# A routed convolution's first two images: sums by identity products, a residual by accumulating transfers, and another order on VectorE

## The chip, the cores and the metric

The kernel runs on one core of a Trainium2 chip. The metric is the device time of one execution in microseconds (us). A core has TensorE (PE, matrix products into PSUM, with PEld for its weight loads), VectorE (DVE), ScalarE (ACT), GpSimd (POOL) and SyncE (SP, here only an issuer of transfers). Each takes its instructions in the order of the program and waits for others on semaphores. Transfers are done by 16 DMA engines that all queues share.

## The reference

Eight images of 128 channels and 64 by 64 pixels go through two layers with residuals. Layer 0 is a modulated deformable 3x3 convolution, batch normalisation and a rectifier. Layer 1, which the change is about, is this:

```python
# --- layer 0 (conv_preact) ---
x = x + _L0_conv_ref(_gn(x), ...)          # ends in relu(yn * gamma + beta)
# --- layer 1 (conv_preact) ---
x = x + _L1_conv_ref(_gn(x), ...)

def _L1_conv_ref(x, ...):
    pooled = jnp.mean(x, axis=(2, 3))
    scores = jax.nn.sigmoid(pooled @ gate_w.T + gate_b)
    ...                                     # top 2 of 4 experts, weights to sum 1
    out = jnp.einsum('ebchw,be->bchw', ye, w_dense)   # ye: a 3x3 convolution by each expert
    return out + _conv2d(x, shared_w) + shared_b[None, :, None, None]
```

The group normalisation `_gn` has 32 groups of 4 channels. As the experts are linear, the kernel mixes their weights per image instead of their outputs, and runs one 3x3 convolution.

## The kernel before

Channels lie on the 128 partitions. `dense()` computes layer 0 band by band and stores its raw output y in DRAM. `layer1()` then goes over the images. Both fix the order of the instructions by hand (`manual_schedule`): what is written first comes first on its engine. SP's and POOL's instructions at the seam of the two layers are also in that order, with loads of layer 1 placed among the last stores of layer 0.

For image b, `load(b)` fetches y and the input x in four quarters each, into one of two pairs of buffers (x1 and xt; for even b the padded images of layer 0 serve). `prepare(b)` is a generator that makes all that the products of image b need, in this order:

- For eight chunks of 512 pixels: the batch normalisation's affine and rectifier on ACT (line 1101), the addition of xt (line 1103; on POOL, and for image 0 the odd chunks on DVE), and the chunk's statistics on DVE (`bn_stats`, line 1105).
- The statistics together (`mv`, line 1110), the group sums as two small products on PE (`pm` line 1113, `pv` line 1123), the scale by a power on POOL, and the gate: a small product `pg` (line 1145) and some fifteen small operations on DVE that end in the experts' weights `wd` (line 1176) and the mixed bias `bmix` (lines 1178 to 1181). Meanwhile ACT writes the normalised chunks into the padded image pad2 (line 1136).
- The mixed weights `wmix` on DVE (line 1212), and u1 and u2 from them (lines 1223 to 1225). The convolution is cut along rows by a transform that computes two output rows from four products (j = 0 to 3): products 0 and 3 use wmix itself, products 1 and 2 use u1 and u2.
- The transformed input v for four groups of 16 rows: transform 1 (line 1191), transform 2 (line 1193), each 528 elements a partition, and transform 0 (line 1195), 1056 elements. Image 0 does its first group's transforms 1 and 2 on POOL.

The main loop runs four products of three matrix products each per group (line 1275, each 128x512 in fp32, two records in the profile), and `collect` takes each result from PSUM: product 1 on ACT, the others on DVE, and a store of 512 KB per group on SP. The 48 matrix products of an image are PE's work of about 42 us. Between the products, `next(ahead_of)` advances `prepare(b + 1)` by one of its turns, nine turns a group. Image 0 is prepared in full before its first product is written down. So DVE does all transforms of image 0, then the statistics of image 1, and the small product pm of image 1 stands on PE's queue behind six products of group 1. For image 0 the first twelve matrix products go column by column of the kernel (kx), each after the weights of its column.

Of the kernel before, what the change touches and what calls it, by code (L numbers as in the profile page):

```python
# [8 lines left out]
F32 = mybir.dt.float32  # L9
I32 = mybir.dt.int32  # L10
AF = mybir.ActivationFunctionType
# [5 lines left out]
P = 128  # L17
# [40 lines left out]
def deform_moe_conv(  # L58
# [104 lines left out]
    most = const.tile([P, B], F32, name="most")  # L163

# [3 lines left out]
    def dense():  # L168

        with ExitStack() as st:  # L170
# [24 lines left out]
            ident = a1.tile([P, P], F32, name="ident")  # L195
# [615 lines left out]
    def general():  # L811

        with ExitStack() as st:
# [12 lines left out]
            ident = a1.tile([P, P], F32, name="ident")  # L826
            make_identity(nc, ident)
# [199 lines left out]
    def layer1():  # L1027
# [6 lines left out]
        with ExitStack() as st:  # L1034
# [8 lines left out]
            ident = b1.tile([P, P], F32, name="ident")  # L1043
            nc.gpsimd.memset(ident, 1.0)
            nc.gpsimd.affine_select(
                out=ident, in_=ident, compare_op=ALU.is_equal, fill=0.0, base=0,
                pattern=[[-1, P]], channel_multiplier=1,
            )
# [13 lines left out]
            def load(b):  # L1062
                if b >= B:
                    return
                x1, xt = x1s[b % 2], xts[b % 2]
                for q in range(4):
                    part = slice(q * HW // 4, (q + 1) * HW // 4)
                    nc.sync.dma_start(out=x1[:, part], in_=ydram[b][:, part])
                    nc.sync.dma_start(out=xt[:, part], in_=x[b, :, part])
                loaded[b] = x1, xt  # L1070
# [22 lines left out]
            def prepare(b, made):  # L1093
# [4 lines left out]
                for c in range(NCH + 2):  # L1098
                    if c < NCH:
                        y = x1[:, c * CH : (c + 1) * CH]  # L1100
                        nc.scalar.activation(y, y, AF.Relu, bias=yshift, scale=yscale)  # L1101
                        adder = nc.gpsimd if b or c % 2 == 0 else nc.vector
                        adder.tensor_tensor(y, y, xt[:, c * CH : (c + 1) * CH], ALU.add)  # L1103
                    if c > 1:
                        nc.vector.bn_stats(  # L1105
                            stats[:, c - 2, :], x1[:, (c - 2) * CH : (c - 1) * CH]
                        )
                    yield
                mv = small.tile([P, 2], F32, name="mv")
# [25 lines left out]
                def normalise(c):  # L1135
                    nc.scalar.activation(
                        pad2[:, 1 + 8 * c : 9 + 8 * c, 1 : W + 1],
                        x1[:, c * CH : (c + 1) * CH].rearrange("p (h w) -> p h w", w=W),
                        AF.Identity, bias=shift, scale=scale,
                    )  # L1140
# [36 lines left out]
                mb = small.tile([P, NE], F32, name="mb")  # L1177
                nc.vector.tensor_tensor(mb, eb_sb, wd, ALU.mult)
                bmix = small.tile([P, 1], F32, name="bmix")
                nc.vector.tensor_reduce(bmix, mb, AX.X, ALU.add)  # L1180
                nc.vector.scalar_tensor_tensor(bmix, bmix, sb_sb, gm, ALU.add, ALU.add)
# [21 lines left out]
                if b == 0:  # L1203
                    for c in range(4, NCH):
                        normalise(c)
                    transform(0, 1, nc.gpsimd)
                    transform(0, 2, nc.gpsimd)

                for kx in range(3) if b == 0 else (slice(0, 3),):
# [16 lines left out]
                    if kx == 0:  # L1226
                        transform(0, 0, nc.vector)
                    yield
                for g in range(NG):
                    if b or g:  # L1230
                        transform(g, 1, nc.vector)
                        transform(g, 2, nc.vector)
                        yield
                        transform(g, 0, nc.vector)
                        yield
                made[b] = vs, (wmix[:, 0], u1, u2, wmix[:, 2]), bmix

            made, todo = {}, []
            for _ in prepare(0, made):
                pass  # L1240
            for b in range(B):
                load(b + 2)
                ahead_of = prepare(b + 1, made) if b + 1 < B else iter(())
                vs, us, bmix = made.pop(b)
                for g in range(NG):
                    yo = b2.tile([P, TR, 2, W], F32, name="yo")
                    part = {}

                    def collect(j, pc, g=g, b=b, yo=yo, part=part, bmix=bmix):
# [10 lines left out]
                        elif j == 0:  # L1260
                            nc.vector.tensor_tensor(yo[:, :, 0], pc, part["s"], ALU.add)
                        else:
                            nc.vector.tensor_tensor(yo[:, :, 1], part["d"], pc, ALU.subtract)  # L1263
                            n = 2 * TR * W
                            nc.sync.dma_start(
                                out=out[b, :, g * n : (g + 1) * n],
                                in_=yo.rearrange("p t i w -> p (t i w)"),
                            )
# [13 lines left out]
                    if b == g == 0:  # L1282

                        pcs = {j: ps_m.tile([P, TR, W], F32, name="pc") for j in order}
                        for kx in range(3):
                            for j in order:
                                product(j, kx, pcs[j])
# [73 lines left out]
```

## Time and profile before

| | us |
|---|---|
| Median of three runs (1677.96 to 1679.51) | 1678.17 |
| The profiled execution | 1679.23 |
| Its span, first to last instruction | 1677.5 |
| TensorE busy in it | 1575.5 (94%) |
| End of layer 0's last product | 1293.25 |
| First product of layer 1 | 1320.22 |
| End of the last product | 1670.57 |

A row of a timeline reads: start, duration, engine, line of the code, operation, output and inputs by the program's names, shapes, count, and in brackets how long the engine was idle before it and what ended that. In a name such as `pad` or `x` the buffers of image 0 and image 1 can be told: image 0 lies in layer 0's `pad`, image 1 in `x` and `xt`. A table of waits gives total, times and the longest. A row of the windows gives the stretch, its length, busy time of PE, PEld, DVE, ACT and POOL, the granted TensorE clock as a share of full speed, the DMA engines' busy share and GB/s.

### The profile page before, as it was taken

Reading aid. Unit: us, or ns where it says so; the run is one execution under the profiler, and the core shown is the slowest. Engines: PE = TensorE matmul, PEld = TensorE weight load, DVE = VectorE, ACT = ScalarE, POOL = GpSimd, SP = SyncE. Lnnn points to the kernel's source line nnn. Section 1 sums busy time; section 2 is a strip of 40 time slices with the busy share of each in tenths; the row PEclk is TensorE's granted clock in tenths of the full one; section 3 lists DMA queues with packets and bytes.
Section 4 is the critical chain, followed back from the end, with each engine's and each line's share of the span. In section 5 each row is a group of like instructions: output and inputs, shape, how many; then the busy total and the mean of one; then the engine's idle time right before and its main releaser. Section 6 shows DMA issues by size and latency. Waiting matters only on the chain. (4 is left out here: it accounts for less than half of the span.)

```text
span 1677.5 us, 20746 instructions
## 1 busy us (share of the span) xinstructions
PE 1575.5 (94%) x6106; PEld 922.9 (55%) x6106; DVE 1089.8 (65%) x2150; ACT 903.9 (54%) x2096; POOL 956.1 (57%) x1519
## 2 busy tenths in 40 slices
PE   3399999999999999999999999999998489999998
PEld 1265665666566566656665665666665234444443
DVE  5565675666565656756665657565443988888882
ACT  2565764766575557647655755576564333333320
POOL 3475685678577666856775776677771412222210
PEclk9599999999999999999999999999999689999999
DMA  4654863785487468637854874666661634433111
GB/s 135 141 128 104 191 160 97 158 195 135 102 182 173 108 133 202 143 94 157 195 133 103 172 184 116 135 162 152 163 146 48 268 121 150 152 152 145 71 62 53
DMA packets 195668, 235.81 MB, mean 141 GB/s; under 512 B 131765, under 2 KB 146097, under 8 KB 195549
## 3 DMA queue, kind: packets, MB, share of 16 engines
q0 software_dynamic: 94768, 124.63, 33.1%
q1 hardware_dynamic: 100047, 109.38, 21.9%
q8 instruction: 53, 0.87, 0.2%
q14 instruction: 66, 0.54, 0.1%
q10 hardware_dynamic: 734, 0.39, 0.1%
HBM read 183.00 MB, written 50.82 MB: 139 GB/s over the span
## 5 line engine op out<-in xcount | busy, mean ns | idle before, releaser
L663 PE MATMUL pq<-s,xt 100*128 100x324 f32 (+2 forms) x1936 | 677.1, 431 | 18.6 <-DVE s L642 17.7
L678 ACT COPY samples<-pq 128x324 f32<-128x324 f32 (+5 forms) x1144 | 430.6, 400 | 453.8 <-PE pq L663 446.0
L642 DVE TENSOR_TENSOR s<-xwts,ywts 100x324 f32<-100x324 f32 x968 | 452.4, 491 | 318.7 <-PE pq L663 281.7
L689 PE MATMUL py<-samples,dw_sb 128*128 128x384 f32 (+1 forms) x1584 | 629.0, 479 | 6.1 <-ACT y L700 6.0
L588 POOL DMA_DIRECT2D xwts<-tabx x862 | 540.6, 636 | 94.9 <-DMA ywts<-taby 33.6
L572 POOL DMA_DIRECT2D ywts<-taby x526 | 302.3, 587 | 280.3 <-DVE s L642 235.7
L663 PEld LDWEIGHTS pq<-s,xt 100*128 100x128 f32 x1936 | 325.5, 191 | 181.9 <-issue 42.4
L689 PEld LDWEIGHTS py<-samples,dw_sb 128*128 128x128 f32 x1584 | 299.8, 190 | 130.3 <-ACT y L700 13.9
L625 PE MATMUL pt<-ident,picked 128*100 128x128 f32 x968 | 193.2, 275 | 19.7 <-ACT picked L612 19.7
L625 PEld LDWEIGHTS pt<-ident,picked 128*100 128x100 f32 x968 | 124.3, 129 | 146.2 <-issue 67.4
L1275 PE MATMUL pc<-v,u 128*128 128x512 f32 x384 | 172.8, 599 | 9.3 <-DVE u L1224 9.3
L1275 PE MATMUL pc<-v,wmix 128*128 128x512 f32 x384 | 176.6, 606 | 0.0
L632 ACT COPY xt<-pt 100x512 f32<-100x512 f32 (+1 forms) x264 | 147.5, 559 | 1.5 <-PE pt L625 1.4
L703 DVE BATCH_NORM_STATS2 ystats<-y 128x6 f32<-128x384 f32 (+1 forms) x88 | 48.2, 548 | 136.6 <-ACT y L700 136.6
L1275 PEld LDWEIGHTS pc<-v,u 128*128 128x128 f32 x384 | 72.7, 191 | 98.1 <-issue 85.4
L1275 PEld LDWEIGHTS pc<-v,wmix 128*128 128x128 f32 x384 | 72.7, 192 | 88.9 <-issue 85.3
L1253 ACT ACTIVATE t<-pc,bmix 128x512 f32<-128x512 f32 x32 | 22.0, 687 | 183.3 <-PE pc L1275 101.3
L1103 POOL TENSOR_TENSOR x<-x,xt 128x512 f32<-128x512 f32 x32 | 46.5, 1482 | 86.0 <-ACT x L1101 86.0
L604 ACT COPY picked<-pad 128x900 f32<-128x900 f32 x88 | 91.3, 1037 | 4.0 <-DMA xwts<-tabx 4.0
L322 DVE TENSOR_TENSOR combo<-pad 128x1024 f32<-128x1024 f32 x64 | 77.0, 1219 | 17.2 <-PE pc L339 9.7
L1103 POOL TENSOR_TENSOR pad<-pad,pad 128x512 f32<-128x512 f32 x28 | 39.5, 1437 | 71.7 <-ACT pad L1101 71.5
L779 DVE COPY samples<-samples 128x1188 f32<-128x1188 f32 x80 | 61.3, 767 | 0.0
(151 smaller groups left out, 1034.5 us busy)
## 6 DMA issues: line engine op xcount, KB each, us to landing
ywts<-taby POOLq DMA_DIRECT2D x526, 116.0 KB, 4.1
pad<-in_x_dram SPq DMA_DIRECT2D x48, 512.0 KB
xwts<-tabx POOLq DMA_DIRECT2D x172, 116.0 KB, 3.8
out_dram<-yo SPq DMA_DIRECT2D x32, 512.0 KB
xwts<-tabx POOLq DMA_DIRECT2D x173, 92.8 KB, 3.8
yd<-y SPq DMA_DIRECT2D x80, 192.0 KB
xwts<-tabx POOLq DMA_DIRECT2D x172, 69.6 KB, 3.7
pad<-yd SPq DMA_DIRECT2D x16, 512.0 KB
```

Source lines behind the costliest of these rows:

```text
L322: nc.vector.tensor_tensor(combo_of[j][:, half * n : half * n + n], *rows, op)
L572: engine.dma_start(out=y_wts[g % 2][r * Q : (r + NR) * Q, r].rearrange("p a b c -> p (a b c)"), in_=bass.AP(tensor=y_table[b].tensor, offs ...
L588: engine.dma_start(out=x_wts[g % 3][q:QQ:Q, :, lo:hi].rearrange("p t a b c -> p t (a b c)"), in_=bass.AP(tensor=x_table[b].tensor, offset= ...
L604: nc.scalar.copy(picked[g % 2][:, 1 : NT1 - 1], bass.AP(tensor=one.tensor, offset=one.offset, ap=[list(one.ap[0]), [T, NT1 - 2], [W, Q], [ ...
L625: nc.tensor.transpose(pt[0:QQ, c], picked[g % 2][:, c0 + c].rearrange("p y x -> p (y x)"), ident,)
L632: nc.scalar.copy(xts[g][0:QQ, c0 : c0 + n], pt[0:QQ, 0:n])
L642: nc.vector.tensor_tensor(s[0:QQ], x_wts[g % 3][0:QQ, c].rearrange("p a r (y x) -> p (r y) a x", x=3), y_wts[g % 2].rearrange("p r y a x - ...
L663: nc.tensor.matmul(pq[asked], lhsT=xts[g][0:QQ, c], rhs=ss.pop(n)[0:QQ].rearrange("p m a x -> p m (a x)")[asked], start=True, stop=True,)
L678: nc.scalar.copy(rows[:, 6 + m0 : 6 + m1, x, T * c + lo : T * c + hi], by_columns[:, m0:m1, x, lo:hi],)
L689: nc.tensor.matmul(py[:, first:], lhsT=dw_sb[:, 3 * ky + kx], rhs=samples[g % 2][:, first + ky : T + ky, 2 - ky, 2 - kx, kx : kx + W], sta ...
L1103: adder.tensor_tensor(y, y, xt[:, c * CH : (c + 1) * CH], ALU.add)
L1275: nc.tensor.matmul(pc, lhsT=us[j][:, kx], rhs=vs[g][:, rows, kx : kx + W], start=(kx == 0), stop=(kx == 2),)
```

## The change

- Layer 1 uses layer 0's identity matrix (now in the constants) and builds none of its own.
- Image 0: chunks 2, 4, 6 and 7 are summed on PE, as a product of the identity with xt and one with the rectified chunk, in PSUM; the statistics and the normalisation read them there. Chunks 0, 1, 3 and 5 are added on DVE. POOL adds none.
- Image 1: x is not loaded into xt; after each pair of rectified chunks POOL issues a transfer that adds x to them in place. All eight statistics come in one place, before group 2's transforms of image 0.
- Image 0's first group: transform 0 on POOL, 1 and 2 on DVE; the first twelve products go in the order 0, 3, 1, 2.
- bmix is computed after the weights.
- Image 0's `prepare` is not run to its end: the transforms of groups 2 and 3 are dealt out between image 1's turns (`merged`).
- The loads of image b + 2 are issued in group 1, not ahead of group 0.
- The very last store is split in two halves, the second issued from ACT.

```diff
+    ident = const.tile([P, P], F32, name="ident")
...
                     nc.sync.dma_start(out=x1[:, part], in_=ydram[b][:, part])
-                    nc.sync.dma_start(out=xt[:, part], in_=x[b, :, part])
+                    if b != 1:
+                        nc.sync.dma_start(out=xt[:, part], in_=x[b, :, part])
...
-                for c in range(NCH + 2):
-                    if c < NCH:
-                        y = x1[:, c * CH : (c + 1) * CH]
-                        nc.scalar.activation(y, y, AF.Relu, bias=yshift, scale=yscale)
-                        adder = nc.gpsimd if b or c % 2 == 0 else nc.vector
-                        adder.tensor_tensor(y, y, xt[:, c * CH : (c + 1) * CH], ALU.add)
-                    if c > 1:
-                        nc.vector.bn_stats(
-                            stats[:, c - 2, :], x1[:, (c - 2) * CH : (c - 1) * CH]
+                if b == 0:
+                    relus = list(chunks)
+                    summed = (2, 4, 6, 7)
+                    for c in summed:
+                        pc = ps_m.tile([P, TR, W], F32, name="pc")
+                        chunks[c] = pc.rearrange("p h w -> p (h w)")
+                        nc.tensor.matmul(
+                            chunks[c], lhsT=ident, rhs=xt[:, c * CH : (c + 1) * CH],
+                            start=True, stop=False,
                         )
+                    for c in range(NCH):
+                        nc.scalar.activation(
+                            relus[c], relus[c], AF.Relu, bias=yshift, scale=yscale
+                        )
+                        if c in summed:
+                            nc.tensor.matmul(
+                                chunks[c], lhsT=ident, rhs=relus[c], start=False, stop=True
+                            )
+                    for c in (0, 1, 3, 5):
+                        add(c, nc.vector)
+                        for done in {1: (0, 1), 3: (2, 3), 5: (4, 5, 6, 7)}.get(c, ()):
+                            count(done)
+                elif b == 1:
+                    for c in range(NCH):
+                        relu(c)
+                        if c % 2:
+                            part = slice((c - 1) * CH, (c + 1) * CH)
+                            nc.gpsimd.dma_start(
+                                out=x1[:, part], in_=x[b, :, part], accum_op=ALU.add
+                            )
                     yield
+                    for c in range(NCH):
+                        count(c)
+                        if c % 2:
+                            yield
...
-                    transform(0, 1, nc.gpsimd)
-                    transform(0, 2, nc.gpsimd)
+                    transform(0, 0, nc.gpsimd)
...
                     if kx == 0:
-                        transform(0, 0, nc.vector)
+                        transform(0, 1, nc.vector)
+                        transform(0, 2, nc.vector)
                     yield
+                mb = small.tile([P, NE], F32, name="mb")
...
+                made[b] = vs, (wmix[:, 0], u1, u2, wmix[:, 2]), bmix
                 for g in range(NG):
...
+            def merged(first, then):
+                wait = None,
+                turns = 2 * wait + (then,) + wait + 2 * (first,) + 5 * wait + 2 * (then,)
+                for turn in turns + 2 * wait + (then,) + 2 * (first,):
+                    if turn:
+                        next(turn)
+                    yield
+                yield from then
...
-            for _ in prepare(0, made):
-                pass
+            first = prepare(0, made)
+            while 0 not in made:
+                next(first)
+            next(first)
             for b in range(B):
-                load(b + 2)
                 ahead_of = prepare(b + 1, made) if b + 1 < B else iter(())
+                if b == 0:
+                    for _ in range(5):
+                        next(ahead_of)
+                    ahead_of = merged(first, ahead_of)
...
+                    if g == 1:
+                        load(b + 2)
...
+                            halves = 2 if b == B - 1 and g == NG - 1 else 1
+                            m = TR // halves
...
-                            for j in order:
+                            for j in (0, 3, 1, 2):
                                 product(j, kx, pcs[j])
```

## The prediction

> **What bounds the kernel now.** I read the page's head first, then the waits of TensorE from 1290 us on, then the timelines of the engines between the two layers, then windows for clock and transfers.
>
> ```profile
> span 1677.5 us, 20746 instructions
> PE 1575.5 (94%) x6106; PEld 922.9 (55%) x6106; DVE 1089.8 (65%) x2150; ACT 903.9 (54%) x2096; POOL 956.1 (57%) x1519
> ```
>
> TensorE (PE) is the bound almost everywhere; what can be won is its idle time. The order of instructions of layer 0 is the same in both kernels, so only the time after 1293 us counts. Who PE waits for there (total, times, longest):
>
> ```profile
> PE pm L1113 <- DVE mv L1110: 23.6, 2, 14.2
> PE pc L1275 <- DVE u L1224: 9.3, 1, 9.3
> ```
>
> The 23.6 us are two waits for statistics: image 0's (14.2) and image 1's. PE's timeline:
>
> ```profile
> 1307.41 0.58 PE L1113 MATMUL pm<-mv,gsel 128*128 128x1 f32 x2 [14.16 <-DVE mv L1110]
> 1320.22 3.75 PE L1275 MATMUL pc<-v,u 128*128 128x512 f32 x4 [9.29 <-DVE u L1224]
> 1326.25 1.88 PE L1275 MATMUL pc<-v,u 128*128 128x512 f32 x4
> 1333.14 5.31 PE L1275 MATMUL pc<-v,u 128*128 128x512 f32 x12
> 1347.90 0.59 PE L1113 MATMUL pm<-mv,gsel 128*128 128x1 f32 x2 [9.44 <-DVE mv L1110]
> 1392.32 0.28 PE L1113 MATMUL pm<-mv,gsel 128*128 128x1 f32 x2
> ```
>
> Products start at 1320.22; six products into group 1, PE stands 9.44 us at pm of image 1 and is full from there on; pm of image 2 comes at 1392.32. A product is two records, 0.862 us at full clock (12 records from 1376.83 to 1381.98 make six). VectorE (DVE):
>
> ```profile
> 1306.98 0.37 DVE L1110 BATCH_NORM_AGGREGATE mv<-stats 128x2 f32<-128x48 f32 x1
> 1314.97 0.61 DVE L1212 SCALAR_TENSOR_TENSOR wmix<-ew_sb,wd,sw_sb 128x384 f32<-128x384 f32 x1
> 1317.58 1.23 DVE L1223 TENSOR_TENSOR u<-wmix 128x128 f32<-128x128 f32 x1
> 1334.59 1.77 DVE L1191 TENSOR_TENSOR v<-pad 128x528 f32<-128x528 f32 x1
> 1375.65 0.70 DVE L1191 TENSOR_TENSOR v<-pad 128x528 f32<-128x528 f32 x1
> 1390.11 0.37 DVE L1110 BATCH_NORM_AGGREGATE mv<-stats 128x2 f32<-128x48 f32 x1
> ```
>
> The same transform takes 0.70 us alone and 1.77 beside GpSimd (POOL), whose adds are these:
>
> ```profile
> 1312.22 1.10 POOL L1191 TENSOR_TENSOR v<-pad 128x528 f32<-128x528 f32 x1 [2.32 <-ACT pad L1136]
> 1317.09 2.83 POOL L1103 TENSOR_TENSOR x<-x,xt 128x512 f32<-128x512 f32 x2 [2.71 <-ACT x L1101]
> 1332.28 10.36 POOL L1103 TENSOR_TENSOR x<-x,xt 128x512 f32<-128x512 f32 x6 [12.36 <-ACT x L1101]
> ```
>
> Windows (granted clock, transfer share and GB/s are the last three columns):
>
> ```profile
> 1297.00:1298.00 1.00, 0.00 (x0) 0.00 (x0) 0.16 (x1) 0.80 (x2) 0.57 (x5) 0.98 0.07 2
> 1310.00:1320.00 10.00, 0.56 (x2) 0.50 (x2) 8.44 (x23) 7.37 (x11) 4.99 (x4) 0.50 1.03 420
> 1342.00:1343.00 1.00, 0.00 (x0) 0.00 (x0) 1.00 (x3) 0.00 (x0) 0.64 (x1) 0.67 0.00 0
> ```
>
> The clock falls to 0.50 about 4.7 us after PE goes idle at 1293.25 and 3.9 us after 1338.46; transfers run full at about 420 GB/s from 1300 to 1327.
>
> **The change, part by part.** All places are in the clock of the trace before; "gain" means earlier.
>
> *Head.* The second identity matrix goes (POOL, 0.20 + 0.28 us), but now lower's two instructions and one border memset stand ahead of yscale on POOL. In the trace four such starts lie at 1296.73, .90, 1297.07, .15: 0.42 us against the one memset's 0.17. Loss 0.25.
>
> *Image 0's sums.* ACT's rectifiers end every 0.707 us, the first at 1298.25 (with the loss). DVE now runs four adds and eight counts at 0.60 each without POOL's: 1298.3 + 7.2 + small waits = 1305.7, against mv at 1306.98: gain 1.28. The four products on xt run from 1293.9 (0.862 each) to 1297.4, the four on rectified chunks from 1299.7, each within 0.95 of its rectifier; the last ends at 1304.4, before count 7 at 1305.1. The pause is 2.3 us, less than the 3.9 after which the clock was seen to fall; at half clock (1.8 each) product 7 would end at 1307 and the gain become a loss of 0.7. I take full clock, and with it 0.3 us less for each of pm and pv (0.28 against 0.58): 0.6. The Trainium skill ("TensorE: Matmul & The Clock Gate", Part 1) lets the clock fall after one idle window of about 3.4 us whose phase runs freely; by it too the 2.3 us stay safe, but the later pauses would be cut earlier than the rows say.
>
> *Gate and first weights.* mb and bmix (0.54 us) leave the path. But POOL's transform of 0 is one instruction of 1056: my estimate is 2.2 us, twice 1.10. It starts after the third normalised chunk, about 1312.8, and ends at 1315.0. DVE's small operations beside POOL end when POOL's ends (wd L1170, begun 1312.53, ended 1313.35; POOL's first transform ended 1313.32), so wd at 1313.1 waits for 1315.0 and the first mix starts 0.1 later than now: between a gain of 0.54 and a loss of 0.1 I take the loss, as two rows show it. First mix: 1314.97 - 1.28 - 0.6 + 0.1 = 1313.2. Four mixes (2.61) to 1315.8; products 0 and 3 need neither u1 nor u2, so PE starts at 1315.9, 4.3 us earlier, and runs 6.0 us for the first four (cold, as now) and 0.862 each after: group 1 at 1328.8, pm of image 1 reached at 1334.0.
>
> *Image 1's residual.* Its eight POOL adds become four accumulating transfers. POOL must issue them after its transform and each pair of rectifiers (pairs end 1315.9 to 1320.2, 1.41 apart). The trace has no accumulating transfer. Bounds: 2.1 MB at 420 GB/s beside the 1.5 MB then left of image 2's load, 8.6 us; at the software queue's rate (124.63 MB in 33.1% of 16 engines' span, 14 GB/s an engine, 224 in all) and that load, 13 us; twice that again for reading the destination, 22 us. From 1317 the last lands at 1326 to 1339. DVE wants it at count 6, 1331.6. I take 1330, the software queue's own rate, hidden; one us later than 1331.6 costs one us. The skill ("DMA: Bandwidth & Descriptors", the fit for one transfer) has 2.0 us plus bytes over 436 GB/s, an estimate of 3.2 us each: the last would land near 1325, and the sum would be the same.
>
> *DVE up to mv of image 1.* From 1315.8: u's 0.86, two transforms 1.24, second column 3.72, third 3.47, bmix 0.54, group 1's transforms 2.41, eight counts 4.78, mv 0.4: 1333.2. PE comes to pm at 1334.0: the stall of 9.44 goes, with the 2.2 us that the cold clock cost after it (six records from 1348.35 took 4.76 instead of 2.59).
>
> *What is late next.* DVE now carries groups 2 and 3's transforms inside PE's time. From mv: s and d 1.2, transforms 2.41, yo 1.2, d/e/gm 0.4, s/d 1.2, yo 0.6, transforms 2.41, yo 0.6, ve 0.15, scale on POOL and back 1.0 = 1344.4; pg is reached by PE at 1344.6. Then score, s, d 1.6, gate 1.96, yo 0.6, three mixes 4.26, yo 0.6, fourth 1.42 = 1355.0. Image 2's first two POOL adds fall here (their rectifiers only wait for group 3's first product): L1220's and the u's work 1.95 plus two waits of 1.07 = 1359.1. bmix 0.54, first transform 0.62 = 1360.3, just when PE begins image 1 (1360.3). In the trace that transform was done at 1369.3, 7.5 us before PE began image 1 (1376.83). Remaining to mv of image 2: two transforms 1.79, s/d 1.2, transforms of groups 1 to 3 7.23, yo 1.2, eight counts 4.78, s/d 1.2, yo 1.2, mv 0.4 = 19.0. Adds 2 to 7 start when ACT has taken image 1's first product, 1363.6, and now lie beside the transforms, not after them: five or six waits of 1.07 (five between 1332 and 1340 show that size), 5.8. mv of image 2: 1385.1. PE reaches its pm at 1375.8 and stands 9.3 us. So the stall moves from image 0 to image 1.
>
> *Later.* pm of image 2 at 1385.2 instead of 1392.32: gain 7.2; the clock is cold again, 2.2 back. From there the order is the old one, with DVE ahead as it was after the old stall. load(b+2) in group 1 leaves SP's issue of image 3 behind one output store; it is needed 25 us later: nothing. If that cover went, ACT would wait for it; no such wait is in sight.
>
> *Tail.* The last store of 512 KB becomes two of 256 on two queues: 0 to 0.6 us (256 KB at 420 GB/s), I take 0.4.
>
> Sum: 7.2 - 2.2 + 0.4 = 5.4. The profiled execution took 1679.23 (span 1677.5 and 1.7 around it), 1.06 above the median 1678.17: 1673.8 against the former, 1672.8 against the latter.
>
> **The rivals.**
> 1. *No second stall, or a short one.* Without contention of adds 2 to 7, mv of image 2 comes at 1379.3, the stall is 3.5 us, and the clock holds (3.9 by the row): gain 13.0 + 0.4, 1664.8. With none at all: 4.3 + 9.44 + 2.2 + 0.4 = 16.3, 1661.8. For it: waits at POOL depend on phase, 0.49 to 1.07. Against: 19.0 us of plain DVE work exceed the 15.5 that PE needs to pm.
> 2. *The accumulating transfers land late (slower).* Place: DVE's counts of image 1, with every transform of groups 2 and 3 queued behind. Break-even 1331.6 + 5.4 = 1337.0; slower by 0.2% from 1340.4. At 1345 the time is 1672.8 + 13.4 = 1686.2. For it: no row prices accumulation, transfers are saturated until 1327. Against: image 2's load shares the line only to about 1325.
> 3. *The identity products run cold.* Sums lose 0.7 instead of gaining 1.28, the 0.6 goes: 1672.8 + 2.6 = 1675.4, no change that can be told.
>
> **How the numbers follow.** A measurement of this kernel can tell about 0.2%, 3.4 us. Chances: main case 0.52 (own range 1670 to 1676.5, from wmix's start and 0 to 2 us of late landing), rival 1 0.24, rival 2 0.12, rival 3 and the like 0.12. Faster by over 0.2% (below 1674.8): 0.24 and most of the main case, 0.44: 0.68. Within: 0.22. Slower: rival 2's part above 1681.5, 0.10. The range leaves out the full 16 us and the late landing: 1663.5 to 1680.
>
> **What would show it.** mv of image 0 at about 1305.7, first product of image 0 near 1315.9 with a cold first four, no wait of PE at pm of image 1, DVE full from 1313 to 1385, transforms of 1.7 us beside POOL adds of image 2, and a wait of 8 to 10 us at pm of image 2. I am wrong if PE waits at pm of image 1 behind counts that wait for a transfer, or if image 2's adds lie elsewhere.

## The result and the profile after

The changed kernel takes 1678.01 us (median of six runs, 1675.37 to 1681.81) against 1678.07 for the kernel before beside it (six runs): ratio 1.0006, 95% interval 0.9989 to 1.0023. A second comparison, told below, gave 1.0006 again, 0.9995 to 1.0017. No change that can be measured came out where 1672.8 was forecast, so about 5 us have to be found. The profiled execution took 1677.45, its span 1675.6.

Layer 0 ended at 1292.80 in this profile and at 1293.25 in the one before, so places are compared as distances from that end. The page's head:

```profile
span 1675.6 us, 20767 instructions
PE 1584.6 (95%) x6122; PEld 924.3 (55%) x6122; DVE 1090.1 (65%) x2152; ACT 903.5 (54%) x2096; POOL 946.0 (56%) x1508
```

TensorE is busy for 9.1 us more than before (1575.5) within a shorter span; the sixteen new records of the identity products are 7.9 of them. TensorE's waits after 1290 us (total, times, longest):

```profile
PE pm L1152 <- DVE mv L1149: 12.3, 3, 8.8
PE pc L1339 <- DVE wmix L1245: 7.2, 1, 7.2
```

Three waits stand at pm: image 0's (1.6), image 1's (1.9, forecast: none) and image 2's (8.8). TensorE's timeline:

```profile
1305.65 0.38 PE L1152 MATMUL pm<-mv,gsel 128*128 128x1 f32 x2 [1.59 <-DVE mv L1149]
1315.69 3.75 PE L1339 MATMUL pc<-v,wmix 128*128 128x512 f32 x4 [7.23 <-DVE wmix L1245]
1335.16 0.38 PE L1152 MATMUL pm<-mv,gsel 128*128 128x1 f32 x2 [1.90 <-DVE mv L1149]
1335.41 7.11 PE L1339 MATMUL pc<-v,wmix 128*128 128x512 f32 x12
1347.73 0.28 PE L1184 MATMUL pg<-gw_sb,pooled 128*128 128x4 f32 x2
1387.96 0.58 PE L1152 MATMUL pm<-mv,gsel 128*128 128x1 f32 x2 [8.82 <-DVE mv L1149]
1388.40 5.47 PE L1339 MATMUL pc<-v,wmix 128*128 128x512 f32 x6
1433.29 0.28 PE L1152 MATMUL pm<-mv,gsel 128*128 128x1 f32 x2
```

The first product starts 22.89 us behind layer 0's end, 4.1 earlier than before (26.97). Twelve records behind the short wait take 7.11 us, where twelve at full clock take 5.3 to 5.4, and six behind the long one 5.47 instead of 2.84. VectorE shows why the waits are there:

```profile
1305.22 0.37 DVE L1149 BATCH_NORM_AGGREGATE mv<-stats 128x2 f32<-128x48 f32 x1
1310.66 2.27 DVE L1215 TENSOR_SCALAR wd<-wd,tot 128x4 f32<-128x4 f32 x1
1327.80 2.46 DVE L1101 BATCH_NORM_STATS2 stats<-x 128x6 f32<-128x512 f32 x4
1330.93 1.29 DVE L1101 BATCH_NORM_STATS2 stats<-x 128x6 f32<-128x512 f32 x2 [0.67 <-DMA x<-in_x_dram]
1333.41 1.29 DVE L1101 BATCH_NORM_STATS2 stats<-x 128x6 f32<-128x512 f32 x2 [1.20 <-DMA x<-in_x_dram]
1334.74 0.37 DVE L1149 BATCH_NORM_AGGREGATE mv<-stats 128x2 f32<-128x48 f32 x1
1348.05 0.16 DVE L1190 TENSOR_TENSOR score<-pg,gb_sb 128x4 f32<-128x4 f32 x1 [1.97 <-PE pg L1184]
1370.13 1.77 DVE L1227 TENSOR_TENSOR v<-pad 128x528 f32<-128x528 f32 x1
1371.82 2.31 DVE L1229 TENSOR_TENSOR v<-pad 128x1056 f32<-128x1056 f32 x1
1387.53 0.37 DVE L1149 BATCH_NORM_AGGREGATE mv<-stats 128x2 f32<-128x48 f32 x1
```

The third and fourth accumulating transfers are waited for (0.67 and 1.20). The transforms of 528 and 1056 elements that lie beside POOL's adds of image 2 take 1.77 and 2.31. Those adds, and the transform that makes wd wait:

```profile
1310.44 2.46 POOL L1229 TENSOR_TENSOR v<-pad 128x1056 f32<-128x1056 f32 x1 [2.70 <-ACT pad L1175]
1367.77 10.87 POOL L1098 TENSOR_TENSOR pad<-pad,pad 128x512 f32<-128x512 f32 x6 [7.38 <-ACT pad L1093]
```

The windows (their columns as before: granted clock, DMA share and GB/s last) put the clock's fall behind the short wait:

```profile
1326.00:1328.00 2.00, 2.00 (x6) 0.81 (x5) 2.00 (x4) 0.69 (x1) 0.00 (x0) 1.00 1.04 254
1328.00:1330.00 2.00, 2.00 (x6) 0.89 (x5) 2.00 (x4) 0.00 (x0) 0.00 (x0) 1.00 1.08 213
1334.00:1335.00 1.00, 0.00 (x0) 0.00 (x0) 0.96 (x3) 0.00 (x0) 0.00 (x0) 1.00 0.00 0
1337.00:1338.00 1.00, 1.00 (x3) 0.42 (x2) 1.00 (x2) 0.00 (x0) 0.00 (x0) 0.50 0.00 0
1340.00:1341.00 1.00, 1.00 (x3) 0.38 (x2) 1.00 (x4) 0.00 (x0) 0.00 (x0) 1.00 0.32 127
```

### The profile page after: what moved, and what is told of

It is laid out like the page before. It is cut to its first block, busy times and chain, and to the rows that moved or that the text cites. A ratio compares the mean times of both kernels' runs of the same rounds, so it can differ in the third digit from the quotient of the medians.

```text
span 1675.6 us, 20767 instructions
## 1 busy us (share of the span) xinstructions
PE 1584.6 (95%) x6122; PEld 924.3 (55%) x6122; DVE 1090.1 (65%) x2152; ACT 903.5 (54%) x2096; POOL 946.0 (56%) x1508
## 5 line engine op out<-in xcount | busy, mean ns | idle before, releaser
L1339 PE MATMUL pc<-v,wmix 128*128 128x512 f32 x384 | 180.1, 615 | 7.2 <-DVE wmix L1245 7.2
L1098 POOL TENSOR_TENSOR x<-x,xt 128x512 f32<-128x512 f32 x24 | 33.2, 1415 | 71.2 <-ACT x L1093 71.2
L1098 POOL TENSOR_TENSOR pad<-pad,pad 128x512 f32<-128x512 f32 x24 | 35.9, 1526 | 66.4 <-ACT pad L1093 66.4
```

The lines of the kernel that those rows point to most:

```text
L1098: engine.tensor_tensor(chunks[c], chunks[c], xt[:, c * CH : (c + 1) * CH], ALU.add)
L1339: nc.tensor.matmul(pc, lhsT=us[j][:, kx], rhs=vs[g][:, rows, kx : kx + W], start=(kx == 0), stop=(kx == 2),)
```

## The experiments

Theory: VectorE is the bound from the gate of image 0 to the statistics of image 2; the gain went to late transfers, to the clock behind two waits, and to POOL's adds of image 2 beside transforms. Rivals are named in each expectation. All places, in us from the end of layer 0 in the same profile:

| kernel | pm of image 0 | first product | pm of image 1 | pm of image 2 | pm of image 3 | last product's end |
|---|---|---|---|---|---|---|
| before | 14.16 | 26.97 | 54.65 | 99.07 | 141.10 | 377.30 |
| before, again | 14.17 | 27.00 | 55.73 | 100.28 | 142.31 | 378.51 |
| after | 12.85 | 22.89 | 42.36 | 95.16 | 140.49 | 376.69 |
| after, again | 13.22 | 23.26 | 42.61 | 93.85 | 138.65 | 374.84 |
| e1 late load | 13.71 | 23.92 | 41.96 | 92.99 | 137.17 | 373.37 |
| e2 accumulate 2 | 13.47 | 23.81 | 41.51 | 87.82 | 132.48 | 368.68 |
| e3 both | 13.23 | 23.26 | 41.00 | 88.52 | 132.60 | 368.80 |
| e4 POOL adds | 13.49 | 24.68 | 51.09 | 102.11 | 146.47 | 382.66 |
| e5 early | 13.29 | 23.34 | 40.75 | 84.20 | 126.33 | 362.53 |
| e6 fill | 12.84 | 22.88 | 42.38 | 93.62 | 135.76 | 371.96 |
| e7 no merge | 13.53 | 23.80 | 46.02 | 100.16 | 145.51 | 381.71 |
| e8 sums | 14.38 | 25.15 | 45.75 | 97.01 | 141.87 | 378.07 |
| e9 transform | 13.62 | 22.87 | 41.35 | 84.58 | 126.72 | 362.92 |
| e10 warm head | 12.85 | 22.45 | 39.88 | 83.31 | 125.45 | 361.65 |

### e1: image 2's load later

```diff
-                    if g == 1:
+                    if g == (2 if b == 0 else 1):
                         load(b + 2)
```

> Image 2's load is issued after the first output store of image 0 (group 2 of image 0 in place of group 1), so the four accumulating transfers of image 1 have the line to themselves. Theory (the transfers land late because image 2's 4.2 MB load shares the line until about 1327, and the clock falls after the 1.9 us that TensorE then waits): the last one lands before 1331, the count waits of 0.67 and 1.20 us go, TensorE waits less than 0.4 us at pm of image 1, the twelve records after it take 5.3 us instead of 7.1, and VectorE's chain brings mv of image 2 forward from 1387.5 to about 1384.5. The wait at pm of image 2 stays 8 to 9.5 us, since it is set by VectorE's work. Time 1675, 3.0 us less than the changed kernel. Rival (the accumulating transfers are limited by their own queue, 213 GB/s, not by the other load): they land at the same 1331 and 1333.4, the wait at pm of image 1 stays 1.9 us, and the time is unchanged, 1678.

Measured: 1675.66, ratio to before 0.9974 (0.9963 to 0.9985). VectorE's counts and TensorE's pm of image 1:

```profile
1328.53 4.84 DVE L1101 BATCH_NORM_STATS2 stats<-x 128x6 f32<-128x512 f32 x8
```

```profile
1334.45 0.28 PE L1152 MATMUL pm<-mv,gsel 128*128 128x1 f32 x2
1334.59 5.44 PE L1339 MATMUL pc<-v,wmix 128*128 128x512 f32 x12
```

All eight counts run in one piece, nothing is waited for at pm, and the clock holds (5.44). Counted from each kernel's first product, pm of image 2 comes 3.2 us earlier than in the changed kernel (69.07 against 72.27), as expected (3.0); the first product itself came 1.0 later here, behind identity products at a granted clock of 0.50. Here the transfers have the line for themselves, and the windows show what they need:

```profile
1322.00:1324.00 2.00, 2.00 (x6) 0.92 (x5) 1.93 (x4) 0.00 (x0) 0.00 (x0) 1.00 1.09 213
1326.00:1328.00 2.00, 2.00 (x6) 0.80 (x5) 2.00 (x4) 0.00 (x0) 0.00 (x0) 1.00 1.09 215
```

All 16 DMA engines are full, at half the 420 GB/s of plain loads. So the rival was half right: here an accumulating transfer holds the line twice as long as a plain load of its bytes, even alone; the shared line made it late on top.

### e2 and e3: image 2's residual by accumulating transfers

```diff
-                    if b != 1:
+                    if b not in (1, 2):
...
                             relu(c)
-                            add(c, nc.gpsimd)
+                            if b == 2:
+                                part = slice((c - 1) * CH, (c + 1) * CH)
+                                if c % 2:
+                                    nc.gpsimd.dma_start(
+                                        out=x1[:, part], in_=x[b, :, part], accum_op=ALU.add
+                                    )
+                            else:
+                                add(c, nc.gpsimd)
```

e3 has e1's edit as well.

> Image 2's residual is added by four accumulating transfers too; GpSimd makes no adds for it, and its second operand is not loaded ahead. Theory (the wait of 8.8 us at pm of image 2 comes from VectorE's transforms standing beside GpSimd's adds, 5.8 us in groups 2 and 3 of image 1 and about 2 us in the weight sums before): the six transforms take 0.70, 0.70, 1.25, 0.70, 0.70, 1.25 us instead of 1.17, 1.77, 2.31, 1.77, 1.77, 2.32, mv of image 2 comes at 1379 to 1380, TensorE waits 0 to 1.5 us there, and 2 to 3 us of cold clock after it go as well: 9 to 11 us less than the changed kernel, 1667 to 1669. Rival (VectorE's plain work is the bound whatever GpSimd does, or the counts now wait for transfers that land late): the transforms get shorter, but the counts wait as long for the transfers, the wait of TensorE stays over 6 us and the time is 1676 to 1679.

> Both edits: image 2's load after the first output store, and its residual by accumulating transfers. If the late landing and the contention are two separate terms, their gains add: no wait over 0.5 us at pm of image 1 nor over 1.5 us at pm of image 2, 12 to 14 us less than the changed kernel, 1664 to 1666. If they are not separate (the chain of VectorE has slack to swallow one of them, or TensorE catches up with it), the time is that of the better one alone, 1667 to 1669.

Measured: e2 1669.42, ratio 0.9939 (0.9925 to 0.9953); e3 1669.47, 0.9935 (0.9921 to 0.9949). VectorE in e2:

```profile
1367.67 0.70 DVE L1234 TENSOR_TENSOR v<-pad 128x528 f32<-128x528 f32 x1
1368.29 1.25 DVE L1236 TENSOR_TENSOR v<-pad 128x1056 f32<-128x1056 f32 x1
1374.63 1.29 DVE L1101 BATCH_NORM_STATS2 stats<-pad 128x6 f32<-128x512 f32 x2 [0.33 <-DMA pad<-in_x_dram]
1378.49 0.69 DVE L1101 BATCH_NORM_STATS2 stats<-pad 128x6 f32<-128x512 f32 x1 [2.57 <-DMA pad<-in_x_dram]
```

With no add beside them all six transforms are back at 0.70 and 1.25: the contention is shown. The wait at pm of image 2 fell from 8.8 to 4.1, not to 1.5, because the counts now waited for transfers (2.9 in all). The gains of e1 and e2 do not add (e3's second outcome): e2 also halves image 2's load, as x is not loaded ahead, and its counts of image 1 already waited for nothing; in e3 the waits for image 2's transfers were 1.65 and 2.46.

### e5: the same, issued early

```diff
+                    for c in range(NCH if b == 2 else 0):
+                        relu(c)
+                        if c % 2:
+                            part = slice((c - 1) * CH, (c + 1) * CH)
+                            nc.gpsimd.dma_start(
+                                out=x1[:, part], in_=x[b, :, part], accum_op=ALU.add
+                            )
                     for c in range(NCH + 2):
-                        if c < NCH:
+                        if c < NCH and b != 2:
```

> Image 2's residual by accumulating transfers as before, but its eight rectifiers and four transfers are issued together, ahead of image 1's first product, so that the rectifiers run from 1356.5 to 1362.2 and not behind image 1's first bias step at 1366. Theory (with the adds gone, the 4.1 us that TensorE still waited at pm of image 2 were counts waiting 0.33 and 2.57 us for transfers that were issued from 1366.3 on): the four transfers, 10 us at 206 GB/s, have landed by 1370, the counts wait for nothing, mv of image 2 comes at about 1376.5 and TensorE, there at 1376.7, waits less than 1 us; the cold clock behind it (5.16 us for six records instead of 2.59) goes too: 6 us less than with the late issue, 1663 to 1664.5, 15 us under the changed kernel. Rival (VectorE's plain work ends at 1380 whatever the transfers do): a wait of 3 to 4 us stays, 1668 to 1669.5.

Measured: 1662.21, ratio 0.9907 (0.9893 to 0.9920), 15.5 us under the kernel before. TensorE:

```profile
1377.97 0.38 PE L1159 MATMUL pm<-mv,gsel 128*128 128x1 f32 x2 [1.04 <-DVE mv L1156]
1378.21 2.84 PE L1346 MATMUL pc<-v,wmix 128*128 128x512 f32 x6
```

The wait is 1.04, six records behind it take the full-clock 2.84, and pm of image 3 comes 14.2 us earlier than in the changed kernel. No count waits for a transfer any more. This is the forecast's first rival made true by other means.

### e4, e7, e8: one part undone each

e4, image 1 (its x is loaded into xt again):

```diff
-                        if c % 2:
-                            part = slice((c - 1) * CH, (c + 1) * CH)
-                            nc.gpsimd.dma_start(
-                                out=x1[:, part], in_=x[b, :, part], accum_op=ALU.add
-                            )
+                        add(c, nc.gpsimd)
```

e7, image 0's `prepare` run to its end ahead of the main loop:

```diff
             next(first)
+            for _ in first:
+                pass
```

e8, image 0, in place of the identity products and VectorE's four adds:

```diff
+                    for c in range(NCH + 2):
+                        if c < NCH:
+                            relu(c)
+                            add(c, nc.vector if c % 2 else nc.gpsimd)
+                        if c > 1:
+                            count(c - 2)
```

> One part undone: image 1's residual by eight GpSimd adds again, right behind the rectifiers, with its second operand loaded ahead; all the rest of the change stays (counts ahead of transforms, sums of image 0 by identity products, order of products). Theory (VectorE is the bound from 1313 us to mv of image 2, and an add of GpSimd beside it costs it 1.07 us): the eight adds cost VectorE 6 to 8.5 us between 1314 and 1330, mv of image 1 comes at 1339 to 1341 instead of 1334.7, TensorE waits 6 to 8 us there and then has a cold clock for 2 us, and everything behind moves by as much: 1682 to 1685. Rival (what the transfers save is lost again in their late landing): mv of image 1 stays within 1 us of 1334.7 and the time is 1677 to 1679.

> One part undone: image 0's transforms of groups 2 and 3 are again ahead of the counts of image 1 on VectorE; all else stays. Theory (VectorE is the bound up to mv of image 2, but image 1's gate needs TensorE to come back from pm in time): the counts start 4.9 us later and no longer wait for transfers, mv of image 1 comes at 1337.5 to 1338 instead of 1334.7, TensorE waits 4.5 to 5 us at pm and is cold behind it, reaches pg of image 1 about 3 us later, and VectorE waits for it: everything behind is 2 to 4 us late, 1680 to 1682. Rival 1 (VectorE's work is the same in sum, so the order within it moves the wait of TensorE from pm of image 2 to pm of image 1 and no more): 1677 to 1679. Rival 2 (the order ahead is worth all of the 4.9 us): 1683 or more.

> One part undone: image 0's residual by eight adds dealt in turn to GpSimd and VectorE, as before the change, in place of four identity product pairs and four adds of VectorE; all else stays. Theory: mv of image 0 comes 0.4 to 1.3 us later (0.4 where the clock has fallen within the identity products, as three of the profiles since show, 1.3 where it has not), pm, pv and pg of image 0 run at half clock (0.58 instead of 0.38 each), and the whole goes 1 to 2 us later: 1679 to 1680, at the edge of what can be told. Rival (the sums are worth nothing, since the gate and the first weights wait for something else): no product of image 0 moves by more than 0.3 us.

Measured: e4 1683.82, ratio 1.0023 (1.0013 to 1.0034); e7 1679.89, 1.0010 (1.0001 to 1.0019); e8 1679.51, 1.0009 (0.9999 to 1.0018). By the table, undoing a part moves pm of image 3 by +6.0 (transfers), +5.0 (counts ahead), +1.4 (sums) against the changed kernel's first profile. The changed kernel's two profiles differ by 1.8 at that place (140.49 and 138.65). So the first two parts do win something in the profile; the 1.4 of the sums lies within that spread and is not shown.

e4 came out at the expected time, in another place: TensorE waited not at pm of image 1 but inside image 0's products, for weights and transforms that VectorE made beside POOL:

```profile
1317.95 3.68 PE L1335 MATMUL pc<-v,wmix 128*128 128x512 f32 x4 [8.07 <-DVE wmix L1241]
1323.38 1.13 PE L1335 MATMUL pc<-v,u 128*128 128x512 f32 x2 [1.75 <-DVE v L1221]
1329.45 3.78 PE L1335 MATMUL pc<-v,wmix 128*128 128x512 f32 x4 [2.24 <-DVE wmix L1241]
```

e7 gave the wait of 4.29 at pm of image 1 that was expected, then 8.23 us for twelve records, and pg of image 1 5.0 us later instead of 3; the profile's 5.0 are the second rival's, while the times allow 0.2 to 3.2 over before. e8's pm of image 0 came 0.7 to 1.5 us later than in the profiles with identity products (expected 0.4 to 1.3), and its pm, pv and pg ran at half clock; its time alone is too near to no change to count on. It holds one more row of use:

```profile
1335.33 0.38 PE L1137 MATMUL pm<-mv,gsel 128*128 128x1 f32 x2 [2.02 <-DVE mv L1134]
1335.57 5.44 PE L1324 MATMUL pc<-v,wmix 128*128 128x512 f32 x12
```

A wait of 2.02 and no fall of the clock, where the changed kernel's first profile fell after 1.90.

### e6: TensorE kept busy in the waits

```diff
+            def fill(n):
+                if n:
+                    idle = ps_m.tile([P, TR, W], F32, name="pc")
+                    for _ in range(n):
+                        nc.tensor.matmul(
+                            idle.rearrange("p h w -> p (h w)"), lhsT=ident,
+                            rhs=ew_sb[:, 0, 0:4].rearrange("p t o -> p (t o)"),
+                            start=True, stop=True,
+                        )
...
+                fill({1: 2, 2: 9}.get(b, 0))
                 pm = ps_s.tile([P, 4], F32, name="pm", tag="pss")
```

> The changed kernel with identity products on constant data that nobody reads, put into TensorE's order directly ahead of pm: two (1.7 us) for image 1 and nine (7.8 us) for image 2. They fill most of the two waits of 1.9 and 8.8 us. Theory (the 7.11 us for twelve records behind the first wait and the 5.47 us for six behind the second are the clock, which falls to 0.50 after these waits): the clock stays at 1.00, the twelve records take 5.3 us and the six 2.8, mv of image 2 comes 1 to 2 us earlier since pg of image 1 is reached earlier, and the time falls by 4 to 5 us, to 1673 to 1674. Rival (the records are long for another reason, or the filling products delay pm by as much as they save): no change, 1677 to 1679.

Measured: 1673.39, ratio 0.9966 (0.9954 to 0.9978).

```profile
1334.26 5.44 PE L1348 MATMUL pc<-v,wmix 128*128 128x512 f32 x12
1376.27 7.89 PE L1089 MATMUL pc<-ew_sb,ident 128*128 128x512 f32 x18
1385.26 0.38 PE L1161 MATMUL pm<-mv,gsel 128*128 128x1 f32 x2 [1.11 <-DVE mv L1157]
1385.51 2.84 PE L1348 MATMUL pc<-v,wmix 128*128 128x512 f32 x6
```

VectorE's work and both waits' causes are untouched; the records behind them are at full clock, pm of image 2 comes 1.5 us earlier and pm of image 3 4.7. That is the clock's price in the changed kernel's first profile; against its second, in which the clock held behind the first wait, pm of image 3 comes 2.9 earlier.

### e9 and e10: the head of image 0, on top of e5

e9:

```diff
-                    transform(0, 0, nc.gpsimd)
...
+                    if b == kx == 0:
+                        transform(0, 0, nc.vector)
```

e10 has that too, makes the products on xt of chunks 4, 6 and 7 twice, and fills behind pg:

```diff
-                        nc.tensor.matmul(
-                            chunks[c], lhsT=ident, rhs=xt[:, c * CH : (c + 1) * CH],
-                            start=True, stop=False,
-                        )
+                        for last in (False, True)[0 if c > 2 else 1 :]:
+                            nc.tensor.matmul(
+                                chunks[c], lhsT=ident, rhs=xt[:, c * CH : (c + 1) * CH],
+                                start=True, stop=not last,
+                            )
...
+                fill(6 if b == 0 else 0)
                 normalise(0)
```

> On top of the early accumulating transfers for image 2, the first transform (of operand 0, group 0 of image 0) goes from GpSimd to VectorE, behind the first column's four mixes. Theory (the small wd operation takes 2.27 instead of 0.23 us because GpSimd's 2.46 us transform runs beside it; on VectorE the transform costs 1.25 us): wd falls to 0.23, the first product of image 0 starts 0.8 us earlier counted from the end of layer 0 (22.5 instead of 23.3 us), and as VectorE is the bound to mv of image 2, the 1.04 us wait there falls to about 0.3 or moves 0.8 earlier with it: 0.8 us in all, 1661 to 1662, less than a measurement of the time can tell. Rival (wd waits for something else, or the transform on VectorE costs as much as it saves): first product within 0.2 us of 23.3.

> The former, and TensorE kept busy before image 0's first product: three of the products on the second operand are made twice in the sums, and six identity products on constant data are put behind pg of image 0 (5.2 us of the 7.2 us that TensorE waits there). Theory: the products on rectified chunks run at full clock (0.95 us each, 0.4 us earlier mv of image 0), and the first four records of image 0 take 1.9 us instead of 3.75, so TensorE reaches pm of image 1 about 2 us earlier; but VectorE, not TensorE, sets mv of images 1 and 2, so TensorE waits 1.5 to 2 us at pm of image 1 and the end moves by no more than 0.4 us: 1660.5 to 1662. Rival (TensorE is the bound from its first product on): pm of image 1 without a wait, and 2 us less, 1659.

Measured: e9 1664.26, ratio 0.9903 (0.9885 to 0.9921); e10 1663.33, 0.9893 (0.9875 to 0.9911). VectorE in e9:

```profile
1312.73 0.23 DVE L1222 TENSOR_SCALAR wd<-wd,tot 128x4 f32<-128x4 f32 x1
1315.49 1.25 DVE L1236 TENSOR_TENSOR v<-pad 128x1056 f32<-128x1056 f32 x1
```

wd falls from 2.27 to 0.23, and from pm to the first product it is 9.25 us instead of 10.05, the 0.8 expected (counted from layer 0's end the first product comes at 22.87, not 22.5); but it did not reach the end: pm of image 2 is 0.4 later than in e5, with a longer cold stretch behind the first product (3.02 instead of 1.92 for the second four records) and a count waiting 0.18 for a transfer. e10's first four records take 1.89, and the wait at pm of image 1 is 0.79, between the two theories; its layer 1 is 1.3 us shorter than e9's. Both times lie above the expected ones; the kernel before took longer beside them too (1680.68, against 1677.73 beside e5). The intervals of e5, e9 and e10 overlap, so none of them is shown best.

### e11 and e12: both kernels once more

No edit.

> The changed kernel once more, unedited, with more timed runs and a second profile. Theory (the profiles show 0.6 us won in layer 1 up to the last product and 0.8 us in the last store, while the end of layer 0 moves by 6 us from profile to profile): 0 to 3 us under the kernel before, ratio 0.998 to 1.000; the wait at pm of image 1 (1.9 us) and at pm of image 2 (8.8 us) come again to within 0.3 us, while the records behind them differ by up to 2 us, as the clock falls at a phase of its own. Rival (the change itself lengthens something outside layer 1, which the first comparison of 1.0006 would hide): a ratio over 1.001 and layer 0's end later than 1296.

> The kernel before once more, unedited, for a second profile of it. From the end of layer 0 to the end of the last product its first profile took 377.3 us, the changed kernel's two 376.7 and 374.8, while the timed comparison says 0.8 us less to 2.9 us more for the changed kernel. Theory (the phase of the clock moves layer 1 by one to two us in either kernel, so that single profiles can't be set against each other below that): this profile gives 374.5 to 376.5, with six records behind the wait at pm of image 1 other than 4.76 us. Rival (layer 1 takes 377.3 again to within 0.3): then the 0.6 to 2.5 us are won in layer 1 in truth, and something outside it takes them back. Time within 0.1% of the kernel before, as it is the same.

Measured: the changed kernel 1679.69, ratio 1.0006 (0.9995 to 1.0017); the kernel before against itself 1679.37, 1.0006 (0.9996 to 1.0016). For the changed kernel both the theory (a ratio of 0.998 to 1.000) and the rival (over 1.001, layer 0's end behind 1296; it was 1293.58) missed. Its second profile has the wait at pm of image 2 again (8.83), but 1.46 instead of 1.90 at pm of image 1, more than the 0.3 of difference expected, and a clock that held behind it:

```profile
1336.19 0.38 PE L1152 MATMUL pm<-mv,gsel 128*128 128x1 f32 x2 [1.46 <-DVE mv L1149]
1336.43 5.44 PE L1339 MATMUL pc<-v,wmix 128*128 128x512 f32 x12
```

That the length of a pause alone does not decide is plainest ahead of image 0's products on rectified chunks (the first profile's row, then the second's):

```profile
1299.25 1.12 PE L1119 MATMUL pc<-pad,ident 128*128 128x512 f32 x2 [2.07 <-ACT pad L1115]
1300.02 5.58 PE L1119 MATMUL pc<-pad,ident 128*128 128x512 f32 x8 [2.07 <-ACT pad L1115]
```

The pause is 2.07 us in both. In the first profile the granted clock stayed at 1.00 and all eight records took 4.8 us, with short pauses between them; in the second it was 0.50 from 1301 to 1304 and they took 5.58. Ten of the profiles have this pause, and the clock fell behind it in eight.

The second profile of before waits 11.54 at pm of image 1, not 9.44, and its layer 1 is 1.2 us longer, so both of e12's expectations missed (a shorter one, and the same to 0.3). The rows trace the extra to a faster start: TensorE's second four records took 1.89 instead of 2.64, POOL's six adds of image 1 began 1.0 us sooner behind layer 0's end, and one more transform of VectorE stood beside them (1.78 instead of 0.70), so mv of image 1 came 1.1 later. From layer 0's end to the last product the changed kernel is 0.6 to 3.7 us shorter over the four pairings, and its last store ends 0.84 earlier. The times do not show that: they allow 0.8 us less to 2.9 more, and a kernel against itself came out at the same 1.0006. Layer 0's end lies anywhere from 1289.6 to 1295.8 in these profiles. The profiled executions are no fair draw either: those of the changed kernel took 1677.45 and 1676.26, below its medians (1678.01 and 1679.69), those of the kernel before 1679.23 and 1680.69, above its own (1678.07 and 1679.37). So the 1.4 to 4.5 us belong to these four executions; whether any of it is there in the mean time stays open.

## Why the prediction was right in part and wrong in part

*Right.* Head: yscale's loss of 0.25 was 0.3. Image 0's sums: mv 12.42 behind layer 0's end, forecast 12.45. That was luck in part: the pause of 2.3 us (2.07 in the trace) that the forecast took for safe let the clock fall in the kernel's second profile and in seven others. wd behind POOL's transform: 2.27, the transform 2.46 against the estimated 2.2. First product forecast at 22.65, measured 22.89; the first four cold. The stall moved on to image 2: forecast 9.3, measured 8.8. Its size fits because two delays offset each other: mv of image 2 ended 3.2 late, and TensorE came to its pm 3.8 late. The six transforms beside adds: 5.8 us, as forecast, and e2 shows it. The Trainium skill ("SBUF — State Buffer", Who interferes with whom) says that a VectorE instruction with two inputs in SBUF contends with a GpSimd instruction that reads SBUF and that the one issued first blocks the other; e2's 0.70 against 1.77 agrees with the first, and no run here tests the second.

*Wrong, first step: "I take 1330, the software queue's own rate, hidden".* The rate was right (205 to 215 GB/s alone in e1 against 224), the cover was not: image 2's load shared the line until about 1328, not 1325, and the last transfer was waited for until 1333.4. The forecast had written that one us later than 1331.6 costs one us; counted from layer 0's end that makes 2.3, and mv of image 1 ended 2.4 late, 1.87 of it in the two waits for transfers. This is what the forecast had named as its sign of being wrong: TensorE waits at pm of image 1 behind counts that wait for a transfer. e1 removes these waits, and nothing else changes in VectorE's order. The forecast's other estimate, 3.2 us for each transfer, did not hold either: alone, in e1, the four took from 1316.2 to about 1328.8.

*Wrong, second step: "the clock holds (3.9 by the row)", and no clock at all at pm of image 1.* The smallest stall after which the trace of before had shown a fall was taken for a threshold. Behind a wait of 1.90 the clock fell at 1336.5 for 3.4 us, and cost 1.8. Image 1's pg came 3.6 later than forecast, VectorE waited 1.97 for it, and mv of image 2 ended 3.2 late. The skill's rule ("TensorE: Matmul & The Clock Gate", Part 1), a fall after at least one idle window of some 3.4 us, would not give it either: TensorE was idle for 1.9 us of the 3.4 before the fall and at work in the rest. In other runs waits of 1.46 and 2.02 passed without a fall, so the length of a wait alone does not decide; that a phase of the clock does would fit, but is not shown.

*Mis-sized: "the clock is cold again, 2.2 back", behind pm of image 2.* 3.3 were lost between pm of image 2 and of image 3. e6 shows the clock as the cause of both clock terms: 4.7 us in one kernel.

*The ledger, first pair of profiles.* Forecast 5.4. pm of image 2 came 3.9 earlier instead of 7.2 (3.3 short; from 1392.32 to 1385.2 it is 7.1, but the forecast's sum has 7.2); the cold clock behind it took 1.1 more; the split tail gave 0.84 instead of 0.4. 5.4 - 3.3 - 1.1 + 0.4 = 1.4, against 0.61 in layer 1 and 0.84 in the tail, 1.45. The times show no gain, which is the open point above: 1678.0 lies outside the main case's own range (1670 to 1676.5), and the forecast had given no change a chance of 0.22. One reading was off without harm: the trace of before shows four waits of 1.07 between 1332 and 1340, not five.

*Rivals.* The second (late transfers) happened in kind, at 1333.4 and far from its break-even of 1337.0. The third (cold identity products) happened in eight of the eleven profiles with such products and cost 0.4 to 0.9 us up to pm of image 0, not 2.6. The first was close on what the contention is worth: with it gone and no wait over 1.1 us at pm (e5, which also loads less for image 2) 15.5 us are won, against 16.3 at most in the forecast.

## What to carry to other kernels

When a part is taken off one engine, price what stands in the new place next to what already runs there: here an accumulating transfer held the DMA line twice as long as a plain load of its bytes, and a plain load beside it made it late. Take the waits that a trace happens to show for examples and not for the shortest that hurts: here stalls near 2 us were followed by a fall of the clock in some profiles and not in others, so a forecast needs both cases. A stall that moves to the next image may have the same cause there: the edit that had helped image 1 was worth more on image 2, once its transfers were issued early enough.

## What the runs showed of the hardware

- Accumulating transfers from DRAM into SBUF ran at 205 to 215 GB/s with the DMA engines full (share 1.03 to 1.09), plain loads at 420; both together at 250 to 287 (windows of one us from 1320 to 1328).
- The clock's low stretch behind the 1.90 us wait lasted 3.4 us (1336.5 to 1339.9). Six records behind waits of 8.8 us took 4.68 to 5.47 us from profile to profile. The same pause of 2.07 us was followed by a fall in eight profiles and not in two.
- An operation on four elements a partition (wd) took 2.27 us beside POOL's 2.46 us transform and 0.23 without it.
- A kernel compared with itself came out at 1.0006, so differences of 1 us of 1678 are not told from nothing here, even with an interval of 0.1% either way.
